# The last scanning phase of a hybrid block, one sequence at a time, with its projection and norm

## The chip, the cores and the metric

One core of one Trainium2 chip. The metric is the device time of one execution in microseconds (us). The engines are named as in the profile: PE is TensorE (PEld its weight loads), DVE is VectorE, ACT is ScalarE, POOL is GpSimd, and SP is the engine whose queue issues all DMA transfers of this kernel. Each engine works through its own instructions in the order in which they were written.

## What is computed

Two sequences of 512 tokens with 512 channels each go through a block-sparse linear layer, a gated feed-forward network, a state-space mixer and the same feed-forward network again, each behind a layer norm and with a residual. All is in float32. Cut to what matters here:

```
x = x + block_sparse(layernorm(x))
x = x + ffn(layernorm(x))              # silu(x@gate) * (x@up) @ down, weights dequantized from integers
x = x + mixer(layernorm(x))
x = x + ffn(layernorm(x))

mixer: gate, hBC, dt = split(x @ in_proj.T)     # 8192 gate channels, 128 heads of 64
  hBC = silu(conv4(hBC)); xs, B, C = split(hBC)
  y   = scan(xs, dt, A, B, C) + D * xs          # in chunks of 128 tokens
  y   = y * rsqrt(mean(y*y over all 8192) + eps) * norm_w * silu(gate)
  out = y @ out_proj.T
```

The factor rsqrt(mean(y*y)) belongs to a token and not to a channel, so the kernel applies it after the projection, when all channels' squares have been summed.

## The kernel before

A tile has 128 partitions. The 1024 tokens are 8 token tiles t; tiles 0 to 3 are sequence b = 0, tiles 4 to 7 sequence b = 1. `x_sb` holds the tokens, `xn_t` the normalized tokens transposed, channels on partitions. PE, ACT and DVE follow the order in which the Python code is written; the queues of POOL and SP are ordered by the framework, each by when its inputs and buffers are due.

**The mixer** (`mixer`, line 416) works on the 64 channel tiles of the scan two at a time: 32 channel pairs. Phase `ph` of the loop at line 846 makes the inputs of pair `ph`, scans pair `ph - 1` and projects pair `ph - 2`. Each pair has four units (j, b): channel tile j of the pair and sequence b. For a unit, `x_tokens` (644) transposes x on PE and multiplies it by dt (DVE, L654) and by the decay (POOL, L658); `states` (666) makes the chunks' states on PE (L671) and carries them on the DVE (L679, L682); `scores` (703) makes for each of two heads a mask m on ACT (L710, L717) and a factor ce (ACT L720, POOL L721); `flush` has the DVE multiply the waiting masks by the chunk's scores (L718). `scan` (724) then multiplies on PE (L729, L738) and returns `gated`, which makes y and the gated result gt on the DVE (L748, L749). `squares` (754) squares y on ACT (L755) and adds it to `sq_acc` on POOL (L756). `out_project` (758) multiplies the gated results of one pair for one token tile (two products of 128x512, L763) and adds the block to the accumulator, which is `x_sb` itself (DVE, L773).

In the last phase (`ph = 32`) there is no new pair to make. In the order before, the units are (0,0), (0,1), (1,0), (1,1). Between their steps stand six blocks of the pair before (`outs`, lines 893 and 910 to 919); the scans of the first two units follow, then the masks of the other two units, their scans (951 to 953), the DVE part of the gate weights of the next slab (955), and the last two blocks. After the loop, from line 999 on, come the eight blocks of the last pair, one per token tile. Among them are the sums of the squares over channels (PE, L1006, with `rsqrt` at 97), and the first two `rest(t)`: `residual` (988) loads a tile of the mixer's input (SP, L990, from the DRAM copy `x_d` into one of three y buffers) and does x = acc * rn + x on the DVE (L991), and `norm` (102) does the statistics (DVE L106, L108) and the square root (ACT L110). `norm` returns a second half, `scaled` (112), that does the reciprocal (L113) and the scaling (L115) on the DVE. `turn` (123) transposes a normalized tile on PE (L128) and copies it into `xn_t` on ACT (L129).

**The second feed-forward** (`ffn`, 319) starts with slab 0 in plain products: for each of four (b, j) a group pg and a group pu (PE, L354), the silu on ACT (L362) and a product on the DVE (L363). A product for sequence b needs all four tiles of that sequence in `xn_t`. After a (b, j) step the loop at 364 takes up to three entries of `waiting`; for the second feed-forward an entry is a norm and turn of one tile of sequence 1. Slabs 1 to 6 (`seven`, 157) use a fast scheme with seven instead of eight products, whose right-hand sides are made from both sequences (`quarters`, 138). Weights are dequantized by `dequant` (204): three loads of 512 KB on SP (L207 to L209), a subtract on the DVE (L212), a multiply on POOL (L213).

**Buffers** set some of the order too: the mask's source `bc` has three buffers, which also hold the gate slab's three loads at the end; m and ce have five each; y three; the PSUM tags "yo" (scan results and projected blocks) three and "tr" (transposes, states, sums) two.

Of the kernel before, what the change touches and what calls it, by code (L numbers as in the profile page):

```python
# [8 lines left out]
F32 = mybir.dt.float32  # L9
I32 = mybir.dt.int32  # L10
# [4 lines left out]
P = 128  # L15
# [22 lines left out]
def kernel(  # L38
# [205 lines left out]
    def block_sparse():  # L244
# [71 lines left out]
        return first, [lambda n=n: turn(n) for n in waiting]  # L316


    def ffn(which, first, waiting, after):


        with tc.tile_pool(name=f"ffn{which}", bufs=1) as pool:
# [93 lines left out]
    def mixer(waiting):  # L416

        with ExitStack() as st:
# [13 lines left out]
            dt = sc.tile([P, NT, H], F32, name="dt")  # L432
            acs = sc.tile([P, NT, H], F32, name="acs")
# [411 lines left out]

            for ph in range(1, n_ph + 1):
                front, last = ph < n_ph, ph >= 2
                c0, c1 = ph * PP, (ph - 1) * PP
# [73 lines left out]
                for k in range(4):  # L922
                    if front:
                        outs(2 * k)
# [5 lines left out]
                    if front:  # L930
                        outs(2 * k + 1)
# [11 lines left out]
                if front:  # L943
                    if ph + 1 < n_ph:
                        wx = load_pair(NCT + c0 + PP, NCT + c0 + PP + 1)
                    gate, later = g_front(wg, gts_new)
# [12 lines left out]
                if front:  # L959
                    if ph > 1:  # L960
                        next(gate)
                    half_scores(0, c0, heads_new)
                    if ph > 1:
                        next(gate)
                    finish(scans)
                    half_scores(1, c0, heads_new)
                    if ph > 1:
                        next(gate)
                    for u in units:
                        silu(xcs_new[u], xcs_new[u])  # L970
                    next(gate)
                    flush()
                    run(gate)
                    for dst, src in later:
                        silu(dst, src)
                    if made:
                        for b in range(2):
                            for x in made[b]:
                                silu(x, x)
                        groups[(c0 + PP) // CTG] = []  # L980
                gts_old, gts, xcs, heads = gts, gts_new, xcs_new, heads_new

            all_squares()


            rn = small.tile([P, NT], F32, name="rn")

# [11 lines left out]
            normed = []  # L999
            for t in range(NT):  # L1000
                out_project(n_ph - 1, [t], gts_old, wo_last)
                if t == 2:
                    ms = psum.tile([P, NT], F32, tag="tr", name="ms")
                    for i in range(NT):
                        b, c = divmod(i, NCH)
                        nc.tensor.matmul(  # L1006
                            ms[:, i : i + 1],
# [100 lines left out]
```

## Time and profile before

| | |
|---|---|
| median of 3 runs | 2360.16 us (2359.36 to 2364.12) |
| the profiled execution's own time | 2362.27 us |
| its span, first to last instruction | 2360.6 us |
| mean granted PE clock | 0.992 |
| PE busy | 2302.2 us (98%) |
| PE weight loads busy | 1211.0 us (51%) |
| DVE busy | 1617.0 us (68%) |
| ACT busy | 1133.7 us (48%) |
| POOL busy | 994.0 us (42%) |
| last phase's first x transposes start | 2014.6 us |
| first product of slab 0 starts | 2074.8 us |
| first product of slab 1 starts | 2116.3 us |

The profile records one execution. A row of a group or of the timeline names a line, an engine, an operation, and out<-in by the program's names. A wait is the idle time of an engine ahead of an instruction, put down to the instruction that released it. A float32 product of 128x512 is recorded as two passes, so "x8" of L763 are four products; the pitch of such passes is 0.43 us at full clock, though each row's mean is 0.59 because they overlap in the pipeline.

### The profile page before, as it was taken

The numbers are of one execution on the slowest core, as the hardware profiler recorded it, in microseconds if no ns is written. First come the engines' busy times: TensorE is split into PE (matmuls) and PEld (weight loads), VectorE is DVE, ScalarE is ACT, GpSimd is POOL, SyncE is SP. The second block draws the span as 40 slices with busy tenths as digits, with TensorE's granted clock in tenths as the row PEclk, the third lists the DMA queues.
The fourth block names the chain that finished last, engine by engine and source line by source line (L and its number), as shares of the span: only waits on it lengthen the run. The fifth ranks groups of instructions, "written<-read, shape, count | busy, mean of one in ns | idle before, by whom it ended". The sixth has DMA issues, their size and how long they took to land. (4 is left out here: it accounts for less than half of the span.)

```text
span 2360.6 us, 27338 instructions
## 1 busy us (share of the span) xinstructions
PE 2302.2 (98%) x9626; PEld 1211.0 (51%) x9626; DVE 1617.0 (68%) x2801; ACT 1133.7 (48%) x2430; POOL 994.0 (42%) x963
## 2 busy tenths in 40 slices
PE   8999998999999999999999999999999999879999
PEld 4444444555555555555555555555555555534444
DVE  6454147877778787877878887777778788745520
ACT  2111026556656565666565656556656565521100
POOL 2663023444454444444354444444444453426600
PEclk9999999999999999999999999999999999989999
DMA  5662012222221222122222222222221222236500
GB/s 183 193 203 91 18 40 90 72 72 64 79 80 60 76 79 74 63 72 81 69 66 81 72 66 79 72 72 67 77 81 61 74 80 63 90 114 216 186 14 22
DMA packets 145576, 201.39 MB, mean 85 GB/s; under 512 B 6944, under 2 KB 91808, under 8 KB 145440
## 3 DMA queue, kind: packets, MB, share of 16 engines
q1 hardware_dynamic: 145440, 199.66, 26.6%
q8 instruction: 76, 1.25, 0.2%
q14 instruction: 60, 0.49, 0.1%
HBM read 194.91 MB, written 4.72 MB: 85 GB/s over the span
## 5 line engine op out<-in xcount | busy, mean ns | idle before, releaser
L165 PE MATMUL proj<-xn_t,w 128*128 128x512 f32 x996 | 464.9, 598 | 7.6 <-ACT ce L720 7.0
L721 POOL TENSOR_TENSOR ce<-ce,c_t 128x384 f32<-128x384 f32 x256 | 269.4, 1056 | 457.5 <-ACT ce L720 456.4
L763 PE MATMUL po<-wo,gt 128*128 128x512 f32 x992 | 436.8, 595 | 0.0
L710 ACT ACTIVATE m<-bc,acs 128x128 f32<-128x128 f32 x1024 | 324.6, 389 | 10.3 <-PE py L729 10.3
L165 PE MATMUL proj<-tq,ws 128*128 128x512 f32 x664 | 308.1, 595 | 9.3 <-DVE xc L554 3.7
L763 PEld LDWEIGHTS po<-wo,gt 128*128 128x128 f32 x992 | 184.6, 190 | 219.6 <-issue 194.9
L165 PEld LDWEIGHTS proj<-xn_t,w 128*128 128x128 f32 x996 | 182.2, 191 | 206.6 <-issue 187.8
L718 DVE TENSOR_TENSOR m<-m,gm 128x512 f32<-128x512 f32 x256 | 219.9, 880 | 2.7 <-ACT m L717 2.7
L554 DVE SCALAR_TENSOR_TENSOR xc<-proj,cw,xc 128x511 f32<-128x511 f32 (+2 forms) x288 | 213.5, 742 | 2.5
L658 POOL TENSOR_TENSOR x_dec<-x_dt,dec 128x384 f32<-128x384 f32 x128 | 129.4, 1021 | 181.8 <-DVE x_dt L654 181.2
L165 PEld LDWEIGHTS proj<-tq,ws 128*128 128x128 f32 x664 | 122.1, 190 | 160.6 <-issue 142.6
L151 POOL TENSOR_TENSOR ws<-w 128x256 f32<-128x256 f32 x96 | 72.5, 755 | 307.3 <-DMA w<-in_win_t_dram 292.7
L405 PE MATMUL ffn_o<-down,h_t 128*128 128x512 f32 x448 | 193.4, 592 | 0.0
L729 PE MATMUL py<-m,x_dt 128*64 128x128 f32 x2048 | 183.4, 277 | 3.1 <-DVE m L718 3.1
L773 DVE TENSOR_TENSOR x_sb<-x_sb,po 128x512 f32<-128x512 f32 x248 | 167.8, 678 | 20.6 <-PE po L763 19.6
L756 POOL TENSOR_TENSOR sq_acc<-sq_acc,y 128x512 f32<-128x512 f32 x128 | 177.1, 1398 | 1.4 <-ACT y L755 1.4
L717 ACT ACTIVATE m<-m 128x512 f32<-128x512 f32 x256 | 161.4, 630 | 7.4
L551 ACT ACTIVATE xc<-proj,cb,cw 128x512 f32<-128x512 f32 x96 | 71.1, 775 | 177.4 <-DVE proj L194 156.5
L165 PE MATMUL proj<-tq,w 128*128 128x512 f32 x332 | 156.0, 592 | 0.0
L165 PE MATMUL proj<-xn_t,ws 128*128 128x512 f32 x332 | 156.0, 592 | 0.0
L738 PE MATMUL py<-ce,state 128*64 128x128 f32 x1536 | 151.7, 274 | 0.0
L729 PEld LDWEIGHTS py<-m,x_dt 128*64 128x64 f32 x2048 | 125.3, 138 | 31.1 <-issue 18.2
(164 smaller groups left out, 3257.8 us busy)
## 6 DMA issues: line engine op xcount, KB each, us to landing
bc<-acs_d SPq DMA_DIRECT2D x128, 512.0 KB, 3.7
w<-in_win_t_dram SPq DMA_DIRECT2D x64, 512.0 KB, 3.8
wo<-in_wo_t_dram SPq DMA_DIRECT2D x31, 512.0 KB, 3.7
wi<-in_gate_w_dram SPq DMA_DIRECT2D x14, 512.0 KB, 3.9
zi<-in_gate_z_dram SPq DMA_DIRECT2D x14, 512.0 KB, 5.1
sf<-in_gate_s_dram SPq DMA_DIRECT2D x14, 512.0 KB, 4.7
wi<-in_up_w_dram SPq DMA_DIRECT2D x14, 512.0 KB, 4.6
zi<-in_up_z_dram SPq DMA_DIRECT2D x14, 512.0 KB, 5.7
```

The lines of the kernel that those rows point to most:

```text
L165: nc.tensor.matmul(ps, lhsT=a[:, kc, :], rhs=b[:, kc, :], start=(start and kc == 0), stop=(stop and kc == KH - 1), skip_group_check=True,)
L405: nc.tensor.matmul(po, lhsT=h_t[:, fc, t * P : (t + 1) * P], rhs=down[:, fc, :], start=(fc == 0), stop=(fc == NFC - 1),)
L554: nc.vector.scalar_tensor_tensor(dst[:, s:], ps[:, : SEQ - s], cw[:, t, 3 - s : 4 - s], dst[:, s:], ALU.mult, ALU.add)
L710: nc.scalar.activation(m[:, c, :], bc[:, hh, c * P : (c + 1) * P], AF.Relu, bias=acs[:, t, h : h + 1], scale=-1.0,)
L717: nc.scalar.activation(m, m, AF.Exp, scale=-1.0)
L718: mults.append(lambda: nc.vector.tensor_mul(m, m, gm))
L721: nc.gpsimd.tensor_mul(ce, ce, c_t[:, P:].rearrange("p (c l) -> p c l", l=P))
L729: nc.tensor.matmul(py[hh * HD : (hh + 1) * HD, c * P : (c + 1) * P], lhsT=x_dt[:, c, hh, :], rhs=m[:, c, :], start=True, stop=(c == 0),)
L738: nc.tensor.matmul(py[hh * HD : (hh + 1) * HD, c * P : (c + 1) * P], lhsT=state[:, c - 1, hh, :], rhs=ce[:, c - 1, :], start=False, stop=True,
L756: nc.gpsimd.tensor_add(sq_acc[:, b, :], sq_acc[:, b, :], y)
L763: nc.tensor.matmul(po, lhsT=gts[j, b][:, c * P : (c + 1) * P], rhs=wo[:, j, :], start=(j == 0), stop=(j == PP - 1),)
L773: nc.vector.tensor_add(acc[:, t, :], acc[:, t, :], po)
```

## The change

The last phase is taken out of the loop (`break` where `not front`) and written out by hand, with the units in the order (0,0), (1,0), (0,1), (1,1), so that both channel tiles of sequence 0 are scanned first. The first two scans come after six blocks of the pair before, then two more blocks, the states of sequence 1, and the last pair's blocks of token tiles 0 to 3 with their own sums of squares (`factors(0)`). Then come the scans of sequence 1; the residuals and norms of tiles 0 to 3 are written between them and the last pair's blocks of tiles 4 to 7; `factors(1)` and the residuals of tiles 4 to 7 end the mixer.

The slab-0 loads of gate and up are both issued ahead of the second scans: the gate's into the `bc` buffers as before, the up's into the buffers of `wo`, `dt` and `acs` (before: into `bc` again, after the gate's). Their DVE and POOL parts come after the blocks of tiles 4 and 5.

In `ffn`, up to two entries of `waiting` are called ahead of a (b, j) step. They do the norms' part of two tiles and return the turns, which are called after that step. For the first feed-forward the entries return the same turns as before, with no work ahead.

```diff
@@ ffn
             for b in range(2):
                 for j in range(2):
                     toks = slice(b * SEQ, (b + 1) * SEQ)
+                    turns = [f() for f in waiting[:2]]
+                    del waiting[:2]
...
                     nc.vector.tensor_mul(h_t[:, j, toks], sg, pu)
-                    for _ in range(3):
-                        if waiting:
-                            waiting.pop(0)()
+                    for f in turns:
+                        f()
@@ mixer
+            def scratch_up(shape):
+                return [
+                    sc.tile(shape, ty, tag=tag, name=nm)
+                    for tag, nm, ty in (("wo", "wi", I32), ("dt", "zi", I32), ("acs", "sf", F32))
+                ]
...
+                if not front:
+
+                    units = [(j, b) for b in range(2) for j in range(PP)]
...
-                if ph == n_ph:
+                if not front:
                     wo_last = load_out(n_ph - 1)
-                if front:
-                    steps = x_front(c0, wx, xcs_new)
-                    wg = load_pair(c0, c0 + 1)
-                else:
-
-                    steps = (outs(k) for k in range(6))
+                    break
+                steps = x_front(c0, wx, xcs_new)
+                wg = load_pair(c0, c0 + 1)
...
-                if not front:
-                    first.append(now(dequant_gate(0, scratch)))
-                    loaded = dequant_up(0, scratch)
-                    for k in range(6, NT):
-                        outs(k)
...
+            def factors(b):
+                ms = psum.tile([P, NCH], F32, tag="tr", name="ms")
+                for c in range(NCH):
+                    nc.tensor.matmul(
+                        ms[:, c : c + 1],
+                        lhsT=sq_acc[:, b, c * P : (c + 1) * P],
+                        rhs=ones[:, 0:1],
+                        start=True,
+                        stop=True,
+                    )
+                rsqrt(rn[:, b * NCH : (b + 1) * NCH], ms, 1.0 / INTER)
...
-            normed = []
-            for t in range(NT):
-                out_project(n_ph - 1, [t], gts_old, wo_last)
-                if t == 2:
...
-                if t == 3:
-                    half = rest(0)
-                if t == 5:
-                    new = rest(1)
-                    normed.append(half())
-                    half = new
-            first.append(now(loaded))
-            for t in range(2, 4):
-                new = rest(t)
-                normed.append(half())
+            def last_outs(t):
+                out_project(n_ph - 1, [t], gts, wo_last)
+
+            tokens(0)
+            tokens(1)
+            outs(0)
+            flush()
+            outs(1)
+            back_scores(2)
+            tokens(2)
+            tokens(3)
+            outs(2)
+            back_scores(3)
+            outs(3)
+            flush()
+            both_states(0)
+            outs(4)
+            outs(5)
+            finish(half_scan(units[:2]))
+            back_scores(4)
+            outs(6)
+            back_scores(5)
+            outs(7)
+            flush()
+            all_squares()
+            both_states(1)
+            back_scores(6)
+            last_outs(0)
+            last_outs(1)
+            flush()
+            back_scores(7)
+            last_outs(2)
+            factors(0)
+            last_outs(3)
+            flush()
+            gate = dequant_gate(0, scratch)
+            up = dequant_up(0, scratch_up)
+            scans = half_scan(units[2:])
+            half = rest(0)
+
+            def ahead(t):
+
+                nonlocal half
+                new = rest(t + 1)
+                normed = half()
                 half = new
-                turn(normed.pop(0))
-            normed.append(half())
-            for t in range(4, NT):
+                return normed
+
+            normed = ahead(0)
+            finish(scans)
+            turn(normed)
+            turn(ahead(1))
+            all_squares()
+            last_outs(4)
+            first.append(now(gate))
+            normed = ahead(2)
+            last_outs(5)
+            turn(normed)
+            first.append(now(up))
+            last_outs(6)
+            normed = half()
+            last_outs(7)
+            turn(normed)
+            factors(1)
+            for t in range(NCH, NT):
                 residual(t)
-            half = norm(4)
-            turn(normed.pop(0))
-            turn(normed.pop(0))
+            half = norm(NCH)
 
             def second(t):
                 nonlocal half
                 new = norm(t + 1) if t + 1 < NT else None
                 normed = half()
                 half = new
-                turn(normed)
+                return lambda: turn(normed)
```

More of the change, by code (lines that the diff above doesn't have):

```diff
@@ L315, in block_sparse @@
             waiting.append(half_f())
-        return first, [lambda n=n: turn(n) for n in waiting]
+        return first, [lambda n=n: lambda: turn(n) for n in waiting]
     def ffn(which, first, waiting, after):
@@ L429, in mixer @@
             nc.sync.dma_start(nw, norm_w)
-            dt = sc.tile([P, NT, H], F32, name="dt")
-            acs = sc.tile([P, NT, H], F32, name="acs")
+            dt = sc.tile([P, NT, H], F32, tag="dt", name="dt")
+            acs = sc.tile([P, NT, H], F32, tag="acs", name="acs")
             dec = sc.tile([P, 2, NCH - 1, H], F32, name="dec")
@@ L922, in mixer @@
                 for k in range(4):
-                    if front:
-                        outs(2 * k)
+                    outs(2 * k)
                     flush()
@@ L929, in mixer @@
                         group_scores(made, groups[c0 // CTG], [k - 1])
-                    if front:
-                        outs(2 * k + 1)
+                    outs(2 * k + 1)
                     drain(1 if k < 3 else 0)
@@ L942, in mixer @@
                     drain()
[L943 to L946, printed above, removed]
+                if ph + 1 < n_ph:
+                    wx = load_pair(NCT + c0 + PP, NCT + c0 + PP + 1)
+                gate, later = g_front(wg, gts_new)
                 if ph == 1:
@@ L953, in mixer @@
                     finish(scans)
-                if not front:
-                    first.append(now(dequant_gate(0, scratch)))
-                    loaded = dequant_up(0, scratch)
-                    for k in range(6, NT):
-                        outs(k)
[L959 to L970, printed above, removed]
-                    next(gate)
[L972 to L980, printed above, removed]
+                if ph > 1:
+                    next(gate)
@@ new lines, in mixer @@
+                half_scores(0, c0, heads_new)
+                if ph > 1:
+                    next(gate)
+                finish(scans)
+                half_scores(1, c0, heads_new)
+                if ph > 1:
+                    next(gate)
+                for u in units:
+                    silu(xcs_new[u], xcs_new[u])
+                next(gate)
+                flush()
+                run(gate)
+                for dst, src in later:
+                    silu(dst, src)
+                if made:
+                    for b in range(2):
+                        for x in made[b]:
+                            silu(x, x)
+                    groups[(c0 + PP) // CTG] = []
@@ L981, in mixer @@
                 gts_old, gts, xcs, heads = gts, gts_new, xcs_new, heads_new
-            all_squares()
             rn = small.tile([P, NT], F32, name="rn")
+            def factors(b):
[9 more added lines that the diff above has]
+                rsqrt(rn[:, b * NCH : (b + 1) * NCH], ms, 1.0 / INTER)
@@ L997, in rest @@
                 return norm(t)
-            normed = []
-            for t in range(NT):
-                out_project(n_ph - 1, [t], gts_old, wo_last)
-                if t == 2:
[L1003 to L1007, printed above, removed]
-                            lhsT=sq_acc[:, b, c * P : (c + 1) * P],
-                            rhs=ones[:, 0:1],
-                            start=True,
-                            stop=True,
-                        )
-                    rsqrt(rn, ms, 1.0 / INTER)
-                if t == 3:
-                    half = rest(0)
-                if t == 5:
-                    new = rest(1)
-                    normed.append(half())
-                    half = new
@@ new lines, in mixer @@
+            flush()
[3 more added lines that the diff above has]
+            last_outs(3)
+            flush()
+            gate = dequant_gate(0, scratch)
[6 more added lines that the diff above has]
+                normed = half()
+                half = new
+                return normed
+            normed = ahead(0)
@@ L1028, in mixer @@
+            finish(scans)
+            turn(normed)
[13 more added lines that the diff above has]
+            for t in range(NCH, NT):
                 residual(t)
-            half = norm(4)
```

## The prediction

> **What bounds the kernel now.** I first read the busy shares and the chain that ended last. TensorE (PE) is busy 98% of the span, and the chain's ends at 2356.8 us run back through PE work alone to about 2116, so time can be won only where PE stands still or runs at a lower clock. Of the 40 slices four have PE below 9 tenths; the two that the change can reach lie side by side, from 2006 to 2124 us: the end of the mixer and the first slab of the second feed-forward. So I cut that stretch into stages, by the view of windows. Columns: stretch, length, busy us of each engine (with instruction counts), granted PE clock, DMA share, GB/s.
>
> ```profile
> core 0: us, PE busy (x) PEld busy (x) DVE busy (x) ACT busy (x) POOL busy (x), PEclk, DMA share, GB/s
> 2014.60:2029.40 14.80, 14.80 (x65) 8.91 (x63) 11.04 (x24) 9.60 (x23) 9.49 (x9) 1.00 0.13 37
> 2029.40:2041.10 11.70, 8.61 (x115) 7.91 (x113) 10.12 (x20) 7.79 (x20) 5.54 (x5) 0.85 0.28 92
> 2041.10:2060.90 19.80, 19.78 (x61) 9.67 (x60) 14.50 (x23) 3.40 (x6) 6.71 (x4) 1.00 0.49 146
> 2060.90:2074.80 13.90, 3.04 (x13) 2.32 (x13) 10.72 (x20) 2.79 (x7) 2.78 (x1) 0.59 0.25 65
> 2074.80:2091.00 16.20, 12.89 (x29) 6.23 (x30) 4.82 (x13) 5.01 (x8) 0.00 (x0) 0.71 0.57 187
> 2091.00:2102.50 11.50, 9.22 (x22) 3.79 (x21) 2.49 (x5) 3.05 (x4) 0.13 (x1) 0.86 0.01 1
> 2102.50:2116.30 13.80, 13.80 (x32) 6.16 (x33) 5.62 (x3) 1.19 (x2) 10.51 (x7) 1.00 0.35 115
> ```
>
> In four of seven stages PE has holes and the clock is at 0.59 to 0.86. The view of waits, PE alone, 2014.6 to 2116.3 us, names who ended the holes:
>
> ```profile
> PE ln_tr L128 <- DVE tmp L115: 9.6, 5, 4.7
> PE pg L354 <- ACT xn_t L129: 5.7, 2, 5.0
> PE py L729 <- DVE m L718: 3.1, 2, 2.9
> PE ln_tr L128 <- DVE rstd L113: 1.2, 1, 1.2
> ```
>
> These are the norms ahead of the transposes (L128), the copy ahead of the first gating, and the masked products ahead of the second scan: 19.6 us. What PE has to do in these 101.7 us (2014.62 to 2116.31, start to start) comes from the timeline's pitches at full clock: four x transposes 1.74, eight blocks of the pair before 13.74 (1.717 each), states 2.68, four scans 6.4 (1.6 each), eight blocks of the last pair 13.74, the sums of squares 1.7, eight turns 3.5 (0.435 each), the first slab 27.5 (eight groups of 3.43): 71.0 us. So 30.7 us are holes (19.6), their drains (some ten, about 0.16 each) and the lower clock (about 9). That is the most the change can win.
>
> **The change, part by part.** I laid out the new order on each engine against the old clock, with the durations of these DVE rows (start, us):
>
> ```profile
> 2063.99 1.46 DVE L115 TENSOR_SCALAR tmp<-x_sb,mv,rstd 128x512 f32<-128x512 f32 x1
> 2065.37 0.74 DVE L991 SCALAR_TENSOR_TENSOR x_sb<-x_sb,rn,y 128x512 f32<-128x512 f32 x1
> 2066.14 0.69 DVE L106 BATCH_NORM_STATS2 stats<-x_sb 128x6 f32<-128x512 f32 x1
> 2066.87 0.18 DVE L108 BATCH_NORM_AGGREGATE mv<-stats 128x2 f32<-128x6 f32 x1
> 2066.97 0.13 DVE L113 RECIPROCAL rstd<-rstd 128x1 f32<-128x1 f32 x1
> 2067.14 0.55 DVE L115 TENSOR_SCALAR tmp<-x_sb,mv,rstd 128x512 f32<-128x512 f32 x1
> ```
>
> By the starts, a residual with its statistics takes 1.6, a reciprocal with its scaling 0.65; a gating (L748, L749) takes 1.45, an accumulate (L773) or mask product (L718) 0.65, a dequant subtract (L212) 1.15, its multiply on POOL (L213) 2.35.
>
> *First sequence early.* Up to the sixth block of the earlier pair (PE at 2028.0) the order is as before, except which unit is second. The first two scans then come at once; their states are ready at 2027.1 and 2028.1. Behind them stand two blocks, the second states, three last-pair blocks, four columns of the sums (0.85), one more block and the second scans: 32.3 us of work, no hole that I find, so PE is through at 2046.9. The mask wait (2.9, with 1.7 of lower clock after it) goes: ACT's last factor is ready at about 2038, the DVE multiplies it at 2044.6 to 2045.2, ahead of its use at 2045.3. That cover is 0.1 us; a DVE late by 1 us costs 1 us there.
>
> *Norms of tokens 0 to 3: the new bound.* The fourth block's accumulate starts at 2043.9; then the DVE has the mask product (to 2045.2), two residuals with statistics (2048.4) and scaling 0 (2049.05). PE, out of work at 2046.9, waits until 2049.2: **2.3 us new**. Turn 0 takes 0.44. Turn 1 is queued on PE ahead of block 4; on the DVE ahead of its input stand two gatings (2.9), residual 2 with statistics (1.6) and scaling 1: 2054.25. PE waits 2049.65 to 2054.4: **4.75 us new**, and blocks 4 and 5, whose inputs are ready at 2052, wait behind turn 1. Row 2's load is issued only after residual 1 (its buffer), at 2047.5; with the landing row of these loads (2.5 to 4.4, median 2.7) it is there by 2050.2 to 2051.9, when it is needed at 2051.9: free, with no margin at the slow end.
>
> Clock: turn 1 and block 4 run at half rate (0.87, 3.43), block 5 partly; block 5 ends at 2061.1. Meanwhile the DVE accumulates block 4 (2059.55), does the gate subtract (2060.7), residual 3 and statistics (2062.4). Scaling 2 then meets the POOL multiply; the row at 2063.99 is that meeting, 1.46 for 0.55, ended 0.3 after POOL's. POOL runs 2061.45 to 2063.8, so scaling 2 ends at 2064.1 (2063.05 without the meeting) and turn 2 starts at 2064.25: **3.15 us new**. Scaling 3 is covered by the half-rate blocks 6 and 7.
>
> Here a rule is weighed. The trace's windows show clock changes at 2036.2, 2039.6, 2063.5, 2080.5, 2087.4 and 2094.2: a grid of 3.41 us. The Trainium skill (TensorE: Matmul & The Clock Gate, "Part 1: The HAM clock gate") also has a free-running window of about 3.4 us, and drops the clock after an idle one. But here the window 2084.0 to 2087.4, with PE busy 1.02 of 3.4 (30%), was followed by half rate, and 2097.6 to 2101.0 (58%) was not. In the new order the window 2060.1 to 2063.5 has 1.0 us of work. By the rule it isn't idle: the clock stays, the sums of squares end at 2070.15. By the nearest row it falls: turn 2, block 6 and most of block 7 at half rate, the end at 2072.45. I take the row, and keep both.
>
> *Second sequence.* The first gating starts at 2072.45 (was 2074.78, and 2.9 slower for the clock) and takes 6.87, to 2079.3. From the sums, the DVE needs 8.55 to scaling 5: rsqrt 0.55, residuals 4 to 6 in 2.0, residual 7 held by its load (issued after residual 4, as before) to 4.75, three statistics, two scalings. Turn 4 is covered; turn 5 waits to 2081.15: 1.4. The next gating ends at 2088.45, turns 6 and 7 at 2089.3, the last copy 0.8 later, then 13.74: slab 1 begins at **2103.85**, against 2116.31.
>
> *Moved loads.* SP now has the slab-0 loads at about 2021 to 2039, needed from 2059.5: hidden by 15 us or more. The three buffers that the up slab borrows come free at 2021 (last x product), 2034.6 (eighth block of the earlier pair) and 2037.4 (last mask's bias), and the queue waits for each in turn. The six slab-1 loads start after residual 7, at about 2077.2 (was 2072.66); before, the DMA share fell 11 us after that start. The gate half is then there by 2083, needed at 2088.7: hidden by 5 us. Table loads are as many as before. After slab 1 nothing differs.
>
> Sum: 2116.31 - 2103.85 = 12.5 us. The profiled execution took 2362.27 (span 2360.6 and 1.7 around it) and would give 2349.8; it lies 2.1 above the median of the runs, 2360.16, so the median becomes 2347.7. A gain in the kernel of over 0.2%, 4.7 us, is what a measurement can tell from no change.
>
> Bounds: the clock's window, +2.3 gain if it stays up, -1.7 if one more window is cold; residual 7's load at 4.4 instead of 2.7, -1.7; more meetings with POOL of the 0.9 kind, up to -2; hand-overs I placed too late or too early, 2 either way. That gives 2343 to 2354 for this case.
>
> **Rivals.** *The DVE chain is shorter than I lay it out, and PE hardly waits.* The three new waits (10.2) and the half rate they bring (about 5) mostly vanish: gain some 25, 2335. For it: before, DVE was 10.7 of 13.9 busy in the worst stage, not full. Against: its rows are measured, and the new order puts gating and norms in one line. 0.10.
>
> *POOL takes the DVE's time.* POOL's two square sums (1.3 each) and two multiplies (2.35) stand in the norm stretch; if all 7.3 land on the DVE chain (1 is counted) and one more window is cold: gain 12.5 - 6.3 - 1.7 = 4.5, 2355.7, the border of no change. For it: L749 took 1.68 for 0.75 beside such sums. Against: most of the chain's rows are fed while POOL is idle. 0.12.
>
> *Slower: row 2's load.* It stands in SP's queue behind the last gate load, which waits for ACT's last factor, and behind 2 MB of weights issued from 2032 on; residual 2 blocks the DVE, thus gating and turn 1. Each microsecond after 2051.9 costs one; from a landing after 2064.4 the kernel loses, and at 2068 gives 2363.8. Against: those loads are issued by 2039, and six took 11 us. 0.04. That the change leaves the order as it was is excluded: the built program's order shows the move on all five queues.
>
> **Numbers.** Likeliest 0.74, at 2347.7; faster 0.87, same 0.09, slower 0.04; range 2341 to 2356, which leaves out most of the first rival and the slower one.
>
> **What to look for.** PE without a hole from 2014.6 to about 2047; then waits of turns 0, 1 and 2 on L115, of about 2, 5 and 3 us; the clock low from 2050 to 2060; the first gating at about 2070 to 2073; slab 1 at about 2104. I am wrong if turn 1 waits less than 2 us (first rival), if residual 2 or 3 waits for a load, or if a scan waits for a mask product again.

## The result and the profile after

| | before | after |
|---|---|---|
| median | 2361.27 us (6 runs, 2359.36 to 2364.12) | 2349.06 us (6 runs, 2348.80 to 2352.01) |
| ratio to before, 95% interval | | 0.9945 [0.9935, 0.9956] |
| the profiled execution's own time | 2362.27 us | 2348.94 us |
| its span | 2360.6 us | 2347.2 us |

The kernel became 12.2 us faster; 2347.7 was forecast. Lines of the changed kernel that are needed here: the scans are L731 and L740, gating L750 and L751, block products L765, accumulate L775, the residual L1001, slab-0 products L357. The norm lines (L106 to L129) and the dequant lines (L212, L213) are unchanged.

I measure every kernel by the same stretch as the prediction, first x transposes of the last phase to first product of slab 1, and split it at the first product of slab 0. All numbers are differences of start times in the PE timeline of each kernel's profiled execution, in us.

| kernel | to the first gating | from there to slab 1 | stretch |
|---|---|---|---|
| before | 60.16 | 41.53 | 101.69 |
| predicted | 57.83 | 31.40 | 89.23 |
| predicted, clock stays up | 55.53 | 31.40 | 86.93 |
| after | 55.42 | 31.54 | 86.96 |

The first half gave 4.7, the second 10.0. The view of windows of the profile after, the stages of the first half (columns as in the prediction: stretch, length, busy us of PE, PEld, DVE, ACT and POOL, granted PE clock, DMA share, GB/s):

```profile
2015.99:2048.70 32.71, 32.70 (x209) 20.20 (x207) 25.26 (x52) 19.27 (x45) 15.90 (x14) 1.00 0.37 114
2048.70:2055.90 7.20, 0.99 (x4) 0.63 (x5) 6.79 (x14) 1.23 (x4) 0.00 (x0) 0.65 0.24 57
2055.90:2065.50 9.60, 6.64 (x12) 3.01 (x12) 4.94 (x8) 1.93 (x4) 5.32 (x3) 0.73 0.30 94
2065.50:2071.40 5.90, 5.45 (x24) 3.21 (x25) 4.12 (x6) 1.17 (x2) 2.35 (x1) 1.00 0.00 0
```

PE runs without a hole for 32.7 us. Then come 7.2 us in which the DVE is busy 6.79 and PE 0.99: there the DVE is the engine that everything waits for. From 2065.5 the clock is full. The view of waits, PE alone, over the same stretch:

```profile
PE ln_tr L128 <- DVE tmp L115: 10.4, 5, 4.1
PE pg L357 <- ACT xn_t L129: 0.7, 1, 0.7
```

Before had 19.6 us of waits of four kinds; the wait for the mask products is gone, and the copy wait fell from 5.7 to 0.7. The timeline shows where the 10.4 lie (start, duration; in brackets the idle time ahead and its releaser):

```profile
2050.78 0.99 PE L128 MATMUL ln_tr<-ident,tmp 128*128 128x128 f32 x4 [2.09 <-DVE tmp L115]
2055.91 1.09 PE L128 MATMUL ln_tr<-ident,tmp 128*128 128x128 f32 x4 [4.14 <-DVE tmp L115]
2056.79 5.76 PE L765 MATMUL po<-w,gt 128*128 128x512 f32 x8
...
2062.36 2.78 POOL L213 TENSOR_TENSOR w<-w,sf 128x1024 f32<-128x1024 f32 x1 [1.51 <-DVE w L212]
2063.97 1.46 DVE L115 TENSOR_SCALAR tmp<-x_sb,mv,rstd 128x512 f32<-128x512 f32 x1
2065.57 0.63 PE L128 MATMUL ln_tr<-ident,tmp 128*128 128x128 f32 x4 [3.01 <-DVE tmp L115]
2066.03 3.60 PE L765 MATMUL po<-w,gt 128*128 128x512 f32 x8
```

Turns 0, 1 and 2 wait 2.1, 4.1 and 3.0 us. Blocks 4 and 5 run mostly at half rate (5.76 us for x8), blocks 6 and 7 at full rate (3.60). Ahead of turn 2 the two engines wait for each other in turn: the DVE first stood idle for 4.68 us until block 4 was done.

### The profile page after: what moved, and what is told of

Its sections match the earlier page's. It is cut to its first block, busy times and chain, and to the rows that moved or that the text cites. A ratio compares the mean times of both kernels' runs of the same rounds, so it can differ in the third digit from the quotient of the medians.

```text
span 2347.2 us, 27338 instructions
## 1 busy us (share of the span) xinstructions
PE 2296.7 (98%) x9626; PEld 1207.3 (51%) x9626; DVE 1614.6 (69%) x2802; ACT 1134.4 (48%) x2431; POOL 993.8 (42%) x963
## 4 chain that ended last, share of the span: by engine, by line
PE 90%; DVE 8%; ACT 1%; issue 0%; DMA 0%; SPq 0%; DVEq 0%; ACTq 0%
PE proj L165 38%; PE po L765 18%; PE ffn_o L407 8%; PE yo L165 6%; PE py L731 4%; PE pst L673 4%; PE py L740 3%; PE x_tr L652 2%; DVE c_t L556 1%; DVE b_t L556 1%; DVE xc L556 1%; PE bs_o L294 1%; PE pg L357 1%; PE pu L357 1%; DVE m L720 1%; PE ln_tr L128 1%
## 5 line engine op out<-in xcount | busy, mean ns | idle before, releaser
L765 PE MATMUL po<-wo,gt 128*128 128x512 f32 x992 | 436.8, 595 | 0.0
L765 PEld LDWEIGHTS po<-wo,gt 128*128 128x128 f32 x992 | 184.6, 190 | 219.6 <-issue 198.0
L775 DVE TENSOR_TENSOR x_sb<-x_sb,po 128x512 f32<-128x512 f32 x248 | 167.9, 678 | 24.6 <-PE po L765 24.0
L731 PE MATMUL py<-m,x_dt 128*64 128x128 f32 x2048 | 181.0, 276 | 0.0
L740 PE MATMUL py<-ce,state 128*64 128x128 f32 x1536 | 149.8, 273 | 0.0
L407 PEld LDWEIGHTS ffn_o<-down,h_t 128*128 128x128 f32 x448 | 84.7, 190 | 104.8 <-issue 104.8
```

Source lines behind the costliest of these rows:

```text
L407: nc.tensor.matmul(po, lhsT=h_t[:, fc, t * P : (t + 1) * P], rhs=down[:, fc, :], start=(fc == 0), stop=(fc == NFC - 1),)
L731: nc.tensor.matmul(py[hh * HD : (hh + 1) * HD, c * P : (c + 1) * P], lhsT=x_dt[:, c, hh, :], rhs=m[:, c, :], start=True, stop=(c == 0),)
L740: nc.tensor.matmul(py[hh * HD : (hh + 1) * HD, c * P : (c + 1) * P], lhsT=state[:, c - 1, hh, :], rhs=ce[:, c - 1, :], start=False, stop=True,
L765: nc.tensor.matmul(po, lhsT=gts[j, b][:, c * P : (c + 1) * P], rhs=wo[:, j, :], start=(j == 0), stop=(j == PP - 1),)
L775: nc.vector.tensor_add(acc[:, t, :], acc[:, t, :], po)
```

## The experiments

The theory to test: after's three new waits come from the DVE, which has gatings, residuals, statistics and scalings of sequence 0 in one line. The rivals: PE's own queue and the lower clock hold the stretch, or the loads and POOL do.

"Part" below means 2015.99 to 2071.41 (to the first gating) or 2071.41 to 2102.95 in after, and the same places in the other kernels. The table gathers them; the runs stand one by one behind it. A ratio is to the kernel before on the same chip.

| run | median us (runs) | ratio, 95% interval | first part | second part | stretch |
|---|---|---|---|---|---|
| feed-forward part alone | 2355.61 (7) | 0.9971 [0.9961, 0.9982] | 60.16 | 33.13 | 93.29 |
| mixer part alone | 2357.31 (18) | 0.9979 [0.9972, 0.9987] | 55.40 | 39.14 | 94.54 |
| block 4 ahead of turn 1 | 2346.92 (5) | 0.9939 [0.9926, 0.9951] | 54.04 | 31.72 | 85.76 |
| weights behind norms | 2348.00 (5) | 0.9940 [0.9927, 0.9952] | 52.78 | 32.77 | 85.55 |
| filled waits | 2348.76 (5) | 0.9935 [0.9923, 0.9948] | 54.22 | 31.51 | 85.73 |
| block and weights | 2344.89 (5) | 0.9920 [0.9906, 0.9933] | 49.79 | 32.78 | 82.57 |
| second scans early | 2346.00 (5) | 0.9925 [0.9912, 0.9937] | 52.29 | 32.03 | 84.32 |
| scans and weights | 2342.11 (5) | 0.9915 [0.9901, 0.9928] | 48.49 | 32.85 | 81.34 |
| thin fill | 2349.79 (2) | 0.9945 [0.9927, 0.9963] | 55.55 | 31.50 | 87.05 |
| after again | 2346.93 (1) | | 55.41 | 31.54 | 86.95 |
| after again, second | 2347.76 (1) | | 56.26 | 31.55 | 87.81 |

A stretch is that of one profiled execution. The three of after differ by 0.86 us, so a difference of 1.2 between two rows is little more than that spread. Of the intervals, only those of "block and weights" and "scans and weights" lie wholly under after's [0.9935, 0.9956]; the medians of the other reorderings can't be told from after's.

### The feed-forward part alone

Before, with only the loop of `ffn` changed.

```diff
+                    turns = [f() for f in waiting[:2]]
+                    del waiting[:2]
...
-                    for _ in range(3):
-                        if waiting:
-                            waiting.pop(0)()
+                    for f in turns:
+                        f()
...
-                turn(normed)
+                return lambda: turn(normed)
```

> The kernel before with the feed-forward part of the change alone (norms of two tiles ahead of a step of slab 0, the turns after it). My theory: the norms of tiles 4 and 5 now run on the DVE beside the first gating, so PE goes from its end at 2084.8 through two turns (0.9) and the second gating (6.87, at full clock since that window has no hole) and two turns and a copy (1.7): 2094.2 where it was 2102.5, 8.3 us less than before. Rival, the gain of the whole change comes from the mixer's order: 0 to 2 us less. Second rival, the norms ahead hold up the first gating's product on the DVE: no gain.

Measured: the first part is before's, to the hundredth (60.16); the second is 33.13 instead of 41.53. All 8.4 us come from issuing the norms of tiles 4 to 7 ahead of the gating that covers them, with the full clock that the second gating then keeps. The mixer's waits, PE over the stretch, stand as they were:

```profile
PE pg L356 <- ACT xn_t L129: 5.7, 2, 5.0
PE ln_tr L128 <- DVE tmp L115: 4.7, 1, 4.7
PE py L730 <- DVE m L719: 3.1, 2, 2.9
```

### The mixer part alone

After, with the old loop of `ffn`.

```diff
-                    turns = [f() for f in waiting[:2]]
-                    del waiting[:2]
...
-                    for f in turns:
-                        f()
+                    for _ in range(3):
+                        if waiting:
+                            waiting.pop(0)()()
```

> The changed kernel with the feed-forward loop as it was (norms and turns of up to three tiles after a step). My theory: the holes of that loop come back, 17.7 us from the end of the first gating's products to the third gating as in the profile before, against 10.5 in the profile after: 7.2 us slower than the changed kernel, some 5 us less than before. Rival, the two parts need each other (the mixer's part alone gains nothing): within 1 us of before. Rival, the mixer's part carries it: 11 us or more less than before.

Measured: the first part is after's (55.40), the second is 7.6 longer. The mixer's new order so gives 4.8 by itself up to the first gating, and 2.4 more because that gating then runs at full clock. Alone the two parts win 8.40 and 7.15, together 14.73: they are nearly additive. The view of waits, PE over the stretch, has eight waits of the same kind in place of after's five:

```profile
PE ln_tr L128 <- DVE tmp L115: 15.4, 8, 4.5
```

### Block 4 ahead of turn 1

If the DVE's one line of gatings and norms is the bound, PE should do what it can earlier: block 4 needs only the gatings, turn 1 needs a residual, statistics and a scaling more.

```diff
-            turn(ahead(1))
-            all_squares()
+            normed = ahead(1)
             last_outs(4)
+            turn(normed)
+            all_squares()
```

> The changed kernel with block 4 of the last pair ahead of turn 1 on PE; the order on every other engine is the same. My theory, PE's own order makes most of the second hole: block 4 starts when the gating ends (2053.6 instead of 2056.8 on the clock of the profile after), its accumulate, the gate's subtract, residual 3 and turn 2 follow 3.1 us earlier: 3 us less than the changed kernel. Rival, the DVE's throughput alone sets the pace: within 0.5 us of the changed kernel.

Measured: turn 1 came when it came in after (39.9 us after the phase's start), as the DVE's line says, and turn 2 came 3.6 us earlier (46.0 for 49.6), as PE's own order says. But the stretch is only 1.2 shorter and not 3. Two rows of the timeline and two windows show who took it back:

```profile
2059.24 2.67 DVE L115 TENSOR_SCALAR tmp<-x_sb,mv,rstd 128x512 f32<-128x512 f32 x1
2059.30 2.33 POOL L213 TENSOR_TENSOR w<-w,sf 128x1024 f32<-128x1024 f32 x1
```

```profile
2057.62:2061.03 3.41, 0.69 (x2) 0.00 (x0) 3.31 (x5) 0.94 (x3) 3.20 (x2) 1.00 0.19 34
2061.03:2064.44 3.41, 2.38 (x6) 1.58 (x7) 3.09 (x3) 0.59 (x1) 2.25 (x3) 0.50 0.48 138
```

The scaling that turn 2 waits for took 2.67 us for 0.55, for the whole of a POOL multiply. In the 3.41 us window of that wait PE was busy 0.69 (20%), and the next window has half clock, so that blocks 6 and 7 took 6.04 us for x8 instead of 3.60: 2.4 given back. This is the cold window that the prediction feared, in another order.

### The weights behind the norms

```diff
-            first.append(now(gate))
             normed = ahead(2)
+            first.append(now(gate))
...
-            first.append(now(up))
             last_outs(6)
             normed = half()
+            first.append(now(up))
```

> The changed kernel with the gate slab's subtract written behind residual 3 and scaling 2, and the up slab's behind scaling 3. My theory, the third hole is the subtract (1.15) and the meeting with the POOL multiply (1.0): turn 2 starts 2.1 us earlier and the first gating 2.7 us earlier, as its weights are ready before it: 2 to 2.7 us less than the changed kernel. Rival, [...]: 1.2 us less. Rival, the weights come too late and the first gating waits: slower than the changed kernel.

Measured: turn 2 waited 0.97 us instead of 3.01 and the scaling ahead of it took 0.55; the first part is 2.6 shorter. The second is 1.2 longer, since now the up multiply runs beside the residuals of tiles 4 to 6 (2.08 us for x3 in after):

```profile
2068.93 2.35 POOL L213 TENSOR_TENSOR w<-w,sf 128x1024 f32<-128x1024 f32 x1 [1.52 <-DVE w L212]
2069.83 3.32 DVE L1001 SCALAR_TENSOR_TENSOR x_sb<-x_sb,rn,y 128x512 f32<-128x512 f32 x3
```

Turn 2's wait fell by 2.04 us: that is the subtract (1.15 in the prediction) and the meeting with the gate's multiply (0.9), so both were on the path at the price forecast. Were the meeting free, only the subtract's 1.15 would have gone, the rival's 1.2. Of the stretch 1.4 us were won, less than the 2 to 2.7 expected.

### The waits filled, the clock kept up

After, with nothing moved, but idle transposes of the identity ahead of turns 0, 1 and 2, into the PSUM tile of the turn: 16, 36 and 24.

```diff
-    def turn(normed):
+    def turn(normed, fill=0):
...
+        for i in range(fill):
+            nc.tensor.transpose(pt[:, i % KC, :], ident, ident)
```

> The kernel after, with nothing moved; only PE does idle transposes of the identity into the PSUM tile of the turn that it is about to do: 16 ahead of turn 0, 36 ahead of turn 1, 24 ahead of turn 2. Nothing that is computed changes. It measures what the lower clock in the stretch is worth by itself. Theory (waits are the DVE's, the clock costs one half-rate stretch of about 9 us, of which the DVE chain hides most): turn 0 and turn 1 come when they came (within 0.3 us of 34.8 and 39.9 us after the phase's start), no window falls to half rate, turn 1 and blocks 4 and 5 run at full rate (x8 of a block 3.6 instead of 5.8 us), turn 2 comes about 2.3 us earlier since its input waits for the accumulate of block 4, and the stretch is 2 to 2.5 us shorter than after's 86.96, so 84.5 to 85; time 2346.5 to 2347. Rival 'the lower clock is most of what is left': 4 us or more shorter, 2345 or less. Rival 'PE's queue is on the path after all': the fillers delay the turns and the stretch is as long or longer.

Measured: turns 0 and 1 came at 34.7 and 39.8, as in after, so the waits are the DVE's and not PE's. The clock fell in no window, block 4 took its full rate, and its accumulate came 2.2 us earlier. But turn 2 came only 1.3 earlier:

```profile
2055.80 3.60 PE L767 MATMUL po<-w,gt 128*128 128x512 f32 x8
2057.20 3.48 POOL L760 TENSOR_TENSOR sq_acc<-sq_acc,y 128x512 f32<-128x512 f32 x2 [16.40 <-ACT y L759]
2059.47 1.75 DVE L1003 SCALAR_TENSOR_TENSOR x_sb<-x_sb,rn,y 128x512 f32<-128x512 f32 x1
```

Moved forward, residual 3 ran into the square sums on POOL and took 1.75 for 0.75. The clock over the 36 transposes of the longest wait stayed full:

```profile
2050.60:2054.80 4.20, 4.17 (x39) 3.93 (x36) 4.02 (x9) 0.73 (x2) 0.00 (x0) 1.00 0.04 13
```

So keeping the clock up made the stretch 1.2 us shorter. With the 1.0 that the meeting took it would be 2.2, within the 2 to 2.5 expected. The median can't be told from after's.

### Block and weights together

Both edits above in one kernel.

> The two earlier moves together: block 4 ahead of turn 1 on PE, and the gate and up subtracts behind the norms of tiles 2 and 3. Alone each made the first half of the stretch 2.6 to 3.5 us shorter, and each lost most of it again to another thing: block first to two half-rate blocks after an emptier clock window, the weights to residuals that met the up multiply on POOL. Theory (the DVE's line is the bound, and what was given back came from the wait that each left): with both, turn 2 follows so early that no window stays under 0.4 busy after the first, turn 2 comes at about 44 us after the phase's start (after: 49.6), the first gating at 49 to 50.5 (after 55.4), and 1 to 2 us are given back to the POOL meeting and residual 7's load: stretch 82 to 83 against after's 86.96, time 2344 to 2345. Rival 'the end is set by residual 7's load and the last norms whatever comes before': stretch 85 to 86 as with each alone, time 2347.

Measured: turn 2 at 43.5, the first gating at 49.8, the stretch 82.57, time 2344.89, all as expected. The longest of PE's waits over the stretch:

```profile
PE ln_tr L128 <- DVE tmp L115: 7.5, 6, 2.1
```

No single wait is over 2.1 us now, and the clock stays full. What "block 4 ahead" gave back alone is not given back here: scaling 2 took 0.61 and the clock fell in no window. What "weights behind norms" gave back still is: the residuals of tiles 4 to 6 again took 3.33 us beside the up multiply, and the second part is 32.78.

### The second scans early

The third scan goes behind block 1 and the fourth behind block 2, so that their gatings lie beside blocks 2 and 3, earlier than the expectation says, and ahead of most of the norms; turns 0, 1 and 2 go behind blocks 5, 6 and 7, and the weights behind the norms of tiles 2 and 3.

```diff
+            scans = half_scan(units[2:3])
+            finish(scans)
+            all_squares()
             last_outs(2)
+            flush()
             factors(0)
-            last_outs(3)
-            flush()
-            scans = half_scan(units[2:])
+            scans = half_scan(units[3:])
...
+            finish(scans)
+            all_squares()
+            last_outs(3)
+            normed = ahead(0)
+            last_outs(4)
+            last_outs(5)
+            turn(normed)
```

> The kernel after with the scans of sequence 1 pulled apart: the third scan follows block 1, the fourth follows block 2 and the sums of sequence 0, and their gatings on the DVE lie beside blocks 3, 4 and 5, ahead of the norms; turn 0 comes after block 5, turn 1 after block 6, turn 2 after block 7; the gate and up subtracts stand behind the norms of tiles 2 and 3. Same work. Theory (the three new waits are there because the DVE's gatings and norms stand in one line while PE has nothing left; PE work left for that time covers them): waits of turns 0 to 2 together under 4 us (after 9.2), clock does not fall or for one window only, first gating at about 46.5 us after the phase's start (after 55.4), stretch 77 to 80 against 86.96, time 2339 to 2342. Rival 'the DVE's line as a whole is the bound': its work in the stretch is the same, waits move to the early blocks (their masks, or the gated results of the last blocks) and the stretch stays at 85 or more. Rival 'masks late': the third scan waits for its mask products by 2 us or more, since those are multiplied one block earlier.

Measured: a miss. Turns 0 to 2 waited 1.6 together, as meant, but the stretch is 84.3 and not 77 to 80. The fourth scan waited 1.2 us for its mask, which was multiplied behind an accumulate and beside a square sum (1.67 for 0.69); the clock fell; and turn 3 waited 3.2 us for a scaling that took 2.00 beside the gate's multiply, whereupon the clock fell again:

```profile
2062.14 2.00 DVE L115 TENSOR_SCALAR tmp<-x_sb,mv,rstd 128x512 f32<-128x512 f32 x1
```

The rival "masks late" named the third scan and 2 us or more; it was the fourth that waited, and for less.

### Scans and weights

The same, with the last masks ahead of block 2's accumulate and the gate's subtract right behind the fourth scan's gating.

```diff
-            last_outs(2)
             flush()
+            last_outs(2)
             factors(0)
...
             all_squares()
+            first.append(now(gate))
             last_outs(3)
...
             normed = ahead(2)
-            first.append(now(gate))
```

> The kernel with the scans of sequence 1 pulled apart, with what that one showed taken out: the last masks are multiplied ahead of block 2's accumulate (there the fourth scan waited 1.2 us for them, behind the accumulate and a square sum on POOL), and the gate's subtract stands right behind the fourth scan's gating, where the DVE idled 1.1 us, so that its POOL multiply runs beside blocks 3 and 4 and no longer beside the scaling of tile 3 (2.0 us for 0.55). The up's subtract stays behind the scaling of tile 3. Same work. Theory (the DVE's line and its meetings with POOL): no wait for masks, no lower clock in the stretch, waits of turns 1 to 3 together 2 to 4 us, first gating at 47.5 to 49.5 us after the phase's start (52.3 without these edits), stretch 78 to 80.5 (84.3 without them, 86.96 after), time 2340 to 2343 against about 2349 to 2350 for after. Rival 'it is given back at the second sequence': the first gating comes as early as that, but turns 4 and 5 wait 3 us or more for the norms behind residual 7's load, and the stretch is 81.5 or more.

Measured: 2342.11 us, the fastest of all. No wait for masks, turns 1 to 3 waited 2.3 together, first gating at 48.5. Two things missed: turn 0 waited 2.5, because the gate's multiply now met residual 1 and scaling 0 (1.16 and 1.45), and the clock fell for one window at 2063.24. The stretch, 81.34, lies between the two theories. The half-rate window made the first gating 1.7 us longer, but that isn't what the stretch lost. Turn 5 waits for the DVE, whose residuals met the up multiply again:

```profile
2063.87 3.33 DVE L1001 SCALAR_TENSOR_TENSOR x_sb<-x_sb,rn,y 128x512 f32<-128x512 f32 x3
2073.21 0.63 PE L128 MATMUL ln_tr<-ident,tmp 128*128 128x128 f32 x4 [0.70 <-DVE tmp L115]
```

"Block and weights" had the first gating at full clock and the same meeting, and its second part is as long (32.78 for 32.85). So the rival "given back at the second sequence" had the mechanism, if not the size: in "block and weights" turns 4 and 5 waited 2.1 together, and here the slower gating covers most of that.

Its interval [0.9901, 0.9928] lies wholly under after's [0.9935, 0.9956]. So there is a version that beats both kernels, by a further 0.3% or so.

### A thin fill: what the clock goes by

As the filled waits, but with 8, 18 and 12 products of one column (two passes each) in place of the transposes.

```diff
+            nc.tensor.matmul(pt[:, i % KC, 0:1], lhsT=ident, rhs=ident[:, 0:1], start=True, stop=True)
```

> The kernel after with fillers ahead of turns 0, 1 and 2 as in the run with filled waits, but of another kind: products of the identity with one column (128x1), 8, 18 and 12 of them (two passes each), which fill PE's time as the profile counts it about as full as the 16, 36 and 24 transposes did. Nothing that is computed changes. It tells what the clock goes by. Theory A (it goes by what the array streams; the profile's busy share overstates one-column products): the clock falls at about 35 us after the phase's start as in after, blocks 4 and 5 take 5.4 to 5.8 us for x8, turn 2 comes at 49 to 50. Rival B (it goes by PE having an instruction in hand): the clock stays, blocks 4 and 5 take 3.6 us, turn 2 comes at 48.0 to 48.6, as with the transposes.

Measured: the clock fell in the middle of the fillers. Two windows of it, and the row of the timeline that has the fillers:

```profile
2049.34:2052.75 3.41, 3.41 (x32) 3.41 (x32) 3.34 (x5) 0.59 (x1) 0.00 (x0) 1.00 0.16 61
2052.75:2056.16 3.41, 3.41 (x16) 3.13 (x16) 1.53 (x5) 0.66 (x2) 0.00 (x0) 0.50 0.24 77
```

```profile
2049.80 5.00 PE L128 MATMUL ln_tr<-ident 128*128 128x1 f32 x36
```

The profile has PE busy for all 3.41 us of the first window, and half clock follows. Blocks 4 and 5 took 5.61 us for x8 and turn 2 came at 49.6, as theory A has it. With transposes of 128 columns in the same place nothing fell. So the clock goes by something that one-column products hardly feed, and not by PE having an instruction in hand. One thing was off: the fall came at 38.1 us after the phase's start, a window later than expected. Without its thin products the window before it was busy 0.42; in "mixer part alone" the clock stayed up after such a window too.

### After, twice again

After was run twice more with a profile, since one step of my sum hung on where the clock's grid lies.

> The kernel after, unchanged, in a further execution with a profile. The clock changes lie on a grid of 3.41 us whose place differs from execution to execution; measured from the phase's start, after's lay at 34.9, 45.1 and 48.6 us. Theory (one step of the sum was decided by that place): if the grid lies so that the window in which block 5 ends has PE busy under about 0.4, the clock falls again there, blocks 6 and 7 take 5.5 us or more for x8 and the stretch is 88.5 to 89.5; else the stretch is 86.5 to 87.5. From the rates on record a grid later than after's by up to 1.5 us gives the fall, an earlier one doesn't. Rival 'the place of the grid is tied to the work': every execution has the same, and the stretch is 86.96 within 0.3.

> As the run before it: the kernel after in a further execution. Theory: stretch 88.5 to 89.5 with a fall at the end of block 5 where the grid's window there is busy under 0.4, else 86.5 to 87.5. Rival: 86.96 within 0.3 each time.

Measured: the first had its fall at 34.9 us after the phase's start, as the first profile had, and the stretch 86.95. In the second it came at 35.4, and a second fall followed at the end of block 5, as predicted of a later grid. Its windows:

```profile
2059.62:2063.03 3.41, 1.16 (x3) 0.19 (x1) 3.31 (x6) 0.29 (x1) 2.71 (x1) 1.00 0.54 154
2063.03:2066.45 3.42, 2.92 (x7) 1.91 (x8) 2.09 (x3) 0.58 (x1) 1.33 (x2) 0.50 0.00 1
```

and the same two of the profile after:

```profile
2061.14:2064.55 3.41, 1.42 (x4) 0.35 (x2) 3.31 (x7) 0.29 (x1) 2.19 (x1) 1.00 0.46 151
2064.55:2067.96 3.41, 2.39 (x9) 1.45 (x10) 2.61 (x4) 0.59 (x1) 1.32 (x2) 1.00 0.15 55
```

1.16 us of work in the window (34%) brings half clock, 1.42 (42%) doesn't. Half a microsecond of the grid's place decides, so the rival that it is tied to the work within 0.3 us falls. But the price was mis-sized by me both times: the stretch is 87.81, 0.85 longer, not 2.

## Why the prediction was right, and the step that was not

In the profiled execution of after the last phase started 1.37 us later than before's (2015.99 for 2014.62). That comes from code that the change doesn't touch: in the windows of 340 to 400 us the granted clock was 0.91 where before had 0.97, at the same PE busy time (52.4 and 52.3). The two repeats of after began the phase at 2014.00 and 2013.97, so the 1.37 belongs to that execution and not to the kernel. With 1.37 added, step by step:

| step | predicted, shifted | measured |
|---|---|---|
| PE out of work, turn 0 | 2048.3, 2050.6 | 2048.7, 2050.78 |
| turn 1 | 2055.8 | 2055.91 |
| half clock falls, rises | about 2051, about 2061 | 2050.90, 2061.14 |
| turn 2, behind a scaling of 1.46 | 2065.6 | 2065.57 |
| next window | half rate | full rate |
| first gating | 2073.8 (clock up: 2071.5) | 2071.41 |
| wait of turn 5 | 1.4 | 0.82 |
| slab 1 | 2105.2 (clock up: 2102.9) | 2102.95 |

**What held.** The mechanism: the mask wait left, the second sequence's norms went under the gating, and in their place came three waits for the DVE, each within 0.7 us of its forecast. That the DVE's single line of gatings, residuals and norms is the new bound of turns 0 and 1 is shown by the filled waits (PE busy, the turns no later) and by block 4 ahead (PE's order changed, turn 1 no earlier). Turn 2 hung on PE's block 4 as well. How much lay in the order of both lines is shown by the kernels that change it: 4.4 us shorter in "block and weights", 5.6 in "scans and weights", with the same work. The meeting of scaling 2 with the gate's multiply was forecast at 1.46, measured 1.46; taking it away, with the subtract, moved turn 2 (weights behind norms).

**What didn't hold: "I take the row, and keep both."** I took the window at the end of block 5 to be busy 1.0 of 3.41 and to bring half clock, at a cost of 2.3. In after it was busy 1.42 and the clock stayed. I had carried the place of the grid over from the execution of before, to a tenth of a microsecond. In after that window began 0.3 us earlier against the phase's start (45.15 for 45.48), in the last run 0.2 later (45.65), and block 5 ended 0.1 later than forecast: that is the 0.4 us of work that the forecast lacked. The choice of the row over the rule was sound in itself: a window that is partly busy does bring half clock (20% in "block 4 ahead", 34% in the last run), though the Trainium skill (TensorE: Matmul & The Clock Gate, "Part 1: The HAM clock gate") asks for an idle one; the same section says, of a kernel's start, that the window's place against the work varies by run, which is what I should have weighed. The price was mis-sized as well: I charged two low windows, the run that fell had one (0.85), since a window busy 2.92 of 3.42 brings full clock back.

**The median, and some luck.** The profiled execution was forecast at 2349.8 and took 2348.94: the clock's term (2.3) less the 1.37 lost in the unmodified part. The median was forecast 2.1 below the profiled execution, as before's lay with three runs; with six it was 1.0 (2361.27 for 2362.27), and after's median lies 0.1 above its profiled execution. That is why the median came out 1.4 us above the forecast, while the stretch won 2.3 more than forecast. Three errors, of 2.3 one way and of 1.4 and 2.2 the other, mostly cancelled: that the median is so near is luck, that the steps are near is not.

**The rivals.** *The DVE chain is shorter*: refuted, turn 1 waited 4.14. *POOL takes the DVE's time*: in after one meeting of 0.9 lies on the path, and another (scaling 3, 1.11 for 0.55) is mostly covered. But the experiments that moved the chain hit further ones, of 0.9 to 2.1 us: as a mechanism it is real, and it is a large part of what "block 4 ahead", "weights behind norms", "filled waits" and "second scans early" gave back. *Row 2's load*: residual 2 started at 2053.45 right behind the gating, with no idle time; the slower side had no ground. Residual 7's load did hold the DVE for 1.4 us, as before.

The wait of turn 5, 0.8 for 1.4, comes out of the trace: the first gating took 7.16 us from start to start for the 6.87 of the forecast, turn 5 started 8.60 after the sums for 8.70, and 0.2 is a matter of counting, since the recorded wait begins only at the recorded end of turn 4 (0.63 for the pitch of 0.435). Not settled: whether the execution at 2352.01, the slowest of after's six, had further low windows (its mean clock is 0.992, the others' 0.994 and 0.995).

## What to carry to other kernels

Find the engine whose line is full in the wait (here the DVE, 6.79 of 7.20 us) and reorder that line, so that what releases the idle engine comes first and what can be late, such as weights for the next stage, comes last; let the idle engine do first what is ready first. Moving one step wins its time only until the next meeting: look for what the moved instruction will now run beside, and move both. Never charge a clock window to a tenth of a microsecond; give it both outcomes, since the grid's place against the work moved by half a microsecond between executions of one kernel.

## What the runs showed of the hardware

The granted clock has two values here, 1.00 and 0.50, and changes only on a grid of 3.41 us: the changes of each trace in this stretch are whole multiples of it apart, for example in before at 2036.2, 2063.5, 2080.5 and 2087.4. The grid's place against the work is not arbitrary: the first line of the grid after the phase's start lies 0.55 to 1.28 us behind that start in twelve of the thirteen traces, and 0.03 us in "block and weights". So an old trace does tell a window's place, to about half a microsecond; why is open.

In the last phase and slab 0 of the traces, the clock fell after windows that the profile has busy up to 0.40 and stayed up after 0.42 and more (after and its repeat, and the mixer part alone). It came back after windows of 0.85 and more, not after 0.74 and less. That is no general threshold. At 385.2 us of after's own trace, far ahead of this stretch, the clock fell after a window busy 0.48 in which eight transposes stood with gaps between them.

The exceptions within the stretch are windows with one-column products: the clock fell after 1.00 in "thin fill", and after 0.64 in "second scans early" and 0.67 in "scans and weights". The last two contain the sums of squares, 0.95 and 0.86 us of 128x1 products. Without them 0.36 and 0.42 are left, under the line and on it; that the sums are the reason was not tried. A busy share is no measure of the clock where such products stand. Closely packed transposes of 128 columns held the clock: in "filled waits" 36 of them bridged 4.1 us at a granted clock of 1.00.

A DVE scaling that meets a POOL multiply doesn't end until the multiply has: in all 44 meetings in the thirteen traces it ended 0.28 to 0.31 us after the multiply, whenever the scaling had begun, in one case 0.06 us ahead of it, so that 0.55 became for example 1.11, 1.46, 2.00 and 2.67. A residual's 0.75 became 1.75 beside square sums. The gate's subtract took 2.29 in "block and weights", where it began during a square sum, and 1.22 in after, where the sums had ended 0.2 us before. Not all DVE work suffers: in after the statistics of tile 3 took their usual 0.69 within the gate's multiply.
